# Two norms by factors spread to all partitions, with taps one a step and softmax sums in their own slot: a two-layer convolution and attention kernel on one core

## Chip, cores and metric

One NeuronCore of a Trainium2 chip. The metric is the device time of one execution in microseconds (us), lower is better. Times are medians over the executions of a kernel. A ratio is the mean time of one kernel's fast runs over the mean of the other's fast runs of the same rounds, so it is not quite the ratio of the medians beside it. Each ratio has a 95% interval.

## The reference

Four images of 128 channels and 64x64 pixels go through two layers. Cut to what matters here:

```python
# layer 0: norm over channels, 3x3 depthwise convolution added, window attention
y = _layernorm2d(x, ln_g, ln_b)            # mean and variance over the 128 channels of a pixel
y = y + _cpe(y, cpe_w, cpe_b)
xw = y.reshape(...)                        # 64 windows of 16x16 pixels
q, k, v = einsum(xw, Wq), einsum(xw, Wk), einsum(xw, Wv)     # 2 branches, 4 heads
attn = softmax(logits over a 5x5 neighbourhood)
x = x + Wo-projected attention output
# layer 1, on tokens [B, 4096, 128]
t = t + linear_attention(layernorm(t))     # running sums over the tokens
t = t + recurrent_ffn(layernorm(t))        # first step: Wx = layernorm(t) @ W.T, then a scan
```

Two norms are touched: the one at the head of layer 0, and the one ahead of `Wx`, called "W's norm" here. In both the mean and the variance are over the channels.

## The kernel before

The image is worked in 16 bands of 16 rows, four windows to a band, so 64 windows. A norm's mean and variance come most easily with pixels on the partitions (rows) and channels along the free axis, but the matmuls want channels on the partitions. So the kernel before scales the rows on VectorE (DVE) and turns them on TensorE (PE):

```python
    def normed(found, tiles, tag):                     # DVE, one instruction for each 128 pixels
        pieces, mv, rs = found
        xn = tiles.tile([P, 4, P], F32, tag=tag, name=tag)
        for j, piece in enumerate(pieces):
            nc.vector.tensor_scalar(
                xn[:, j, :], piece, mv[:, j, 0:1], rs[:, j : j + 1], ALU.subtract, ALU.mult
            )
        return xn

    def turned(xn, j0, n):                             # PE, one transpose for each 128 pixels
        tps = bank()
        for j in range(n):
            nc.tensor.transpose(tps[:, j * P : (j + 1) * P], xn[:, j0 + j, :], ident)
        return tps
...
    def turn_last(h):
        h.xl = p2.tile([P, 512], F32, tag="xl2", name="xl2")
        nc.scalar.copy(h.xl, turned(h.xn, 0, 4))

    def product(h):
        wps = bank()
        nc.tensor.matmul(wps, fwT, h.xl, start=True, stop=True)
        nc.scalar.copy(wx[:, h.b, h.hb], wps.rearrange("p (k s) -> p s k", s=SEG))
```

The softmax sums of a window take two small DMA trips: `dc` gathers 4 rows of sums to all partitions for a quick inverse, `rd` and `rden` send the inverses back and spread them. In the kernel before this is done one window (a "slot" of some 12.5 us) after the exponentials, and the product with the inverses (`oT`) another slot later:

```python
    def weighted(w):                                   # in the slot after the window's logits
        ops, dps = bank(), bank()
        # ... 4 sums of the exponentials on PE into dps
        nc.scalar.copy(den, dps)
        nc.sync.dma_start(dc, den[::HD, :])
        yield
        # ... 24 products with v on PE into ops
        yield
        nc.vector.tensor_tensor(dc, dc, pad_c, ALU.add)          # waits for the DMA of dc
        rc = a2.tile([P, 16], F32, tag="rc", name="rc")
        nc.vector.reciprocal(rc, dc)
        # ... two more small instructions
        nc.sync.dma_start(rd.rearrange("h (a e) -> (h a) e", e=16), rc)
        nc.sync.dma_start(rden, rd.unsqueeze(1).to_broadcast([HEADS, HD, BR * WT]))
```

Instructions of PE, DVE, ScalarE (ACT) and GpSimd (POOL) are held to program order. Those of SyncE (SP), which issues nearly every DMA, are not.

## Time and profile before

| | kernel before |
|---|---|
| time, first runs | 931.11 us (929.38 to 931.3, 3 runs) |
| profiled span, mean granted clock | 925.6 us, 0.981 |
| head (to the start of window 6) | 85.95 us |
| steady part (start of window 6 to that of window 63) | 712.3 us |
| tail (from the start of window 63) | 127.4 us |
| a band in the steady part | 50.2 us |

Windows and bands are counted from 0. The starts are those of the mask matmuls that open each window's logits.

### The profile page before, as it was taken

Reading aid. Unit: us, or ns where it says so; the run is one execution under the profiler, and the core shown is the slowest. Engines: PE = TensorE matmul, PEld = TensorE weight load, DVE = VectorE, ACT = ScalarE, POOL = GpSimd, SP = SyncE. Lnnn points to the kernel's source line nnn. Section 1 sums busy time; section 2 is a strip of 40 time slices with the busy share of each in tenths; the row PEclk is TensorE's granted clock in tenths of the full one; section 3 lists DMA queues with packets and bytes.
Section 4 is the critical chain, followed back from the end, with each engine's and each line's share of the span. In section 5 each row is a group of like instructions: output and inputs, shape, how many; then the busy total and the mean of one; then the engine's idle time right before and its main releaser. Section 6 shows DMA issues by size and latency. Waiting matters only on the chain.

```text
span 925.6 us, 26464 instructions
## 1 busy us (share of the span) xinstructions
PE 876.4 (95%) x10508; PEld 655.1 (71%) x10508; DVE 730.4 (79%) x2408; ACT 540.1 (58%) x1010; POOL 260.8 (28%) x358
## 2 busy tenths in 40 slices
PE   4978999999999999999999999999999999977894
PEld 3856777877777877777787777777777878665452
DVE  6464979888798878798888889787879887578684
ACT  3655656565756565665657575666666565623563
POOL 2122141423232232304132323323230412121195
PEclk9988999999999999999999999999999999989898
DMA  4112121122212121212112121212121111153254
GB/s 122 26 46 62 38 70 49 47 59 63 60 55 60 54 57 49 74 38 68 49 51 60 60 60 49 62 45 73 49 70 39 55 37 50 41 210 132 86 219 150
DMA packets 53189, 63.46 MB, mean 69 GB/s; under 512 B 22976, under 2 KB 33856, under 8 KB 52416
## 3 DMA queue, kind: packets, MB, share of 16 engines
q1 hardware_dynamic: 51616, 61.10, 21.1%
q8 instruction: 85, 1.39, 0.6%
q10 hardware_dynamic: 1440, 0.57, 0.2%
q14 instruction: 48, 0.39, 0.1%
HBM read 35.44 MB, written 17.30 MB: 57 GB/s over the span
## 4 chain that ended last, share of the span: by engine, by line
PE 61%; DVE 24%; ACT 5%; POOL 4%; issue 3%; DMA 2%; ACTq 0%; POOLq 0%; DVEq 0%; SPq 0%
PE bank L343 8%; DVE y L294 8%; PE bank L471 7%; PE bank L388 6%; PE bank L218 6%; PE bank L500 5%; PE bank L406 4%; PE bank L356 4%; PE bank L418 4%; PE bank L608 3%; DVE st L197 2%; PE z L834 2%; PE bank L579 2%; PE bank L543 2%; PE bank L581 2%
## 5 line engine op out<-in xcount | busy, mean ns | idle before, releaser
L294 DVE SCALAR_TENSOR_TENSOR y<-ypad,cpe_w,y 128x512 f32<-128x512 f32 x240 | 189.8, 791 | 17.1 <-ACT y L292 13.6
L397 ACT ACTIVATE es<-bank 128x512 f32<-128x512 f32 x256 | 132.2, 602 | 77.0 <-PE bank L388 77.0
L446 POOL TENSOR_TENSOR oT<-o_sb,rden 128x512 f32<-128x512 f32 x64 | 83.9, 1311 | 242.7 <-DMA rden<-rd 138.4
L201 POOL TENSOR_SCALAR rs<-mv 128x4 f32<-128x4 f32 (+2 forms) x100 | 25.1, 251 | 366.5 <-DVE mv L199 163.2
L209 DVE TENSOR_SCALAR xn<-x,mv,rs 128x128 f32<-128x128 f32 x256 | 89.9, 412 | 26.6 <-POOL rs L202 26.6
L202 POOL TENSOR_TENSOR rs<-rs,mhalf 128x4 f32<-128x4 f32 (+2 forms) x100 | 106.3, 1063 | 8.3
L388 PEld LDWEIGHTS bank<-q,k 32*128 32x128 f32 x3072 | 97.7, 189 | 7.5 <-ACT k L351 6.3
L388 PE MATMUL bank<-q,k 32*128 32x96 f32 (+1 forms) x3072 | 96.3, 270 | 1.1 <-ACT k L351 1.1
L418 PEld LDWEIGHTS bank<-es,v_sb 128*32 128x32 f32 x3072 | 56.6, 110 | 30.2 <-issue 20.2
L471 PE MATMUL bank<-woT,oT 128*128 128x128 f32 x512 | 68.0, 289 | 5.8 <-POOL oT L446 5.8
L471 PEld LDWEIGHTS bank<-woT,oT 128*128 128x128 f32 x512 | 64.8, 202 | 9.9 <-POOL oT L446 7.5
L500 PE MATMUL bank<-xl,awT 128*128 128x512 f32 x128 | 70.0, 630 | 0.0
L418 PE MATMUL bank<-es,v_sb 128*32 128x96 f32 (+1 forms) x3072 | 69.9, 239 | 0.0
L406 PE MATMUL bank<-es,ones 128*32 128x512 f32 x512 | 69.1, 612 | 0.0
L363 ACT COPY v_sb<-bank 128x512 f32<-128x512 f32 x64 | 37.6, 587 | 53.6 <-PE bank L356 44.6
L343 PE MATMUL bank<-y2w,wqT 128*128 128x256 f32 x256 | 67.3, 386 | 1.0 <-DVE y2w L294 1.0
L343 PE MATMUL bank<-y2w,wkT 128*128 128x256 f32 x256 | 66.7, 384 | 0.0
L356 PE MATMUL bank<-wvT,y2w 128*128 128x256 f32 x256 | 66.0, 380 | 0.0
L351 ACT COPY q<-bank 128x512 f32<-128x512 f32 x64 | 37.7, 588 | 42.2 <-PE bank L343 40.2
L351 ACT COPY k<-bank 128x512 f32<-128x512 f32 x64 | 37.4, 584 | 37.6 <-PE bank L343 37.5
L197 DVE BATCH_NORM_STATS2 st<-x 128x6 f32<-128x128 f32 x256 | 55.5, 280 | 1.1
L343 PEld LDWEIGHTS bank<-y2w,wqT 128*128 128x128 f32 x256 | 46.0, 195 | 13.0 <-issue 7.2
(118 smaller groups left out, 1713.7 us busy)
## 6 DMA issues: line engine op xcount, KB each, us to landing
rden<-rd SPq DMA_DIRECT2D x64, 256.0 KB
v_sb<-v_sb SPq DMA_DIRECT2D x128, 64.0 KB
resd<-rs_o SPq DMA_DIRECT2D x32, 256.0 KB
out<-ot SPq DMA_DIRECT2D x32, 256.0 KB
xin<-in_xt SPq DMA_DIRECT2D x15, 512.0 KB
res<-resd SPq DMA_DIRECT2D x3, 2048.0 KB
late<-resd SPq DMA_DIRECT2D x2, 1024.0 KB
dc<-den SPq DMA_DIRECT2D x64, 8.0 KB
```

The source lines that it names most:

```text
L202: nc.gpsimd.tensor_tensor(rs[:, :n], rs[:, :n], mhalf[:, :n], ALU.pow)
L209: nc.vector.tensor_scalar(xn[:, j, :], piece, mv[:, j, 0:1], rs[:, j : j + 1], ALU.subtract, ALU.mult)
L294: nc.vector.scalar_tensor_tensor(y2, src, cpe_w[:, tap : tap + 1], y2, ALU.mult, ALU.add)
L343: nc.tensor.matmul(pps[:, br * WT : (br + 1) * WT], wT[:, br * P : (br + 1) * P], y2, start=True, stop=True,)
L356: nc.tensor.matmul(vps[:, e * 256 : (e + 1) * 256], y2[:, e * P : (e + 1) * P], wvT, start=True, stop=True,)
L388: nc.tensor.matmul(sps[h][:, cols], w["k"][rows, k0 : k0 + P], w["q"][rows, cols], start=False, stop=(br, n) == pieces[-1],)
L397: nc.scalar.activation(es, sps[h], AF.Exp, scale=scale)
L406: nc.tensor.matmul(dps[rows], ones[:, :HD], w["es", h], start=True, stop=True)
L418: nc.tensor.matmul(ops[rows, cols], w["v"][:, n, c0 : c0 + HD], w["es", h][:, cols], start=(br, n) == pieces[0], stop=(br, n) == pieces[-1],)
L446: nc.gpsimd.tensor_tensor(oTs[n][:, :, :, wj * WS : (wj + 1) * WS], w["o"].rearrange("p (a r c) -> p a r c", a=BR, c=WS), w["rden"].rearra ...
L471: nc.tensor.matmul(yps[:, j * P : (j + 1) * P], oT[:, br, t], woT[:, br, :], start=br == 0, stop=br == BR - 1,)
L500: nc.tensor.matmul(zps, awT[:, m * P : (m + 1) * P], h.xl, start=True, stop=True)
```

## The change

The intent is to take the turning of layer 0's rows and of W's rows off PE, and their scaling off DVE. The host hands over x a second time with channels on the partitions (`xc`). The factors (1/sigma and mean/sigma of each pixel) are measured on rows as before, sent to DRAM, and read back spread to all 128 partitions. POOL then multiplies and subtracts on `xc`. W's norm needs only 1/sigma, as the mean is taken out by centring the weights once; the W product runs on the residual stream that is turned anyway, and DVE multiplies the result with the spread 1/sigma. Beside this: one tap of the convolution a step (a step is one of the 21 small portions into which the work ahead on a band is cut), where the second half of a band had two; sums in the window's own slot; SP in the program order too; the last, unused states dropped; six buffers for `ys`. The core of the diff:

```diff
-ENGINES = [... for e in ("PE", "DVE", "Activation", "Pool")]
+ENGINES = [... for e in ("PE", "DVE", "Activation", "Pool", "SP")]
...
+    class Group:                       # up to 4 x 128 pixels of a band
+        def measure(self):
+            # ... bn_stats, bn_aggr on DVE, three small POOL instructions -> self.both [P, 2, 4]
+            nc.sync.dma_start(self.x[:, : self.k * P], ins["xc"][b, wi, :, ...])
+        def send(self):
+            self.there = dram4.tile([2, P, self.k], F32, tag=f"both_d{self.k}", name="both_d")
+            nc.sync.dma_start(self.there.rearrange("f p j -> p f j"), self.both[:, :, : self.k])
+        def spread(self):
+            nc.sync.dma_start(
+                self.all[:, :, : self.k * P],
+                self.there.rearrange("f p j -> f (p j)").partition_broadcast(P),
+            )
+        def scale(self):
+            nc.gpsimd.tensor_tensor(x, x, self.all[:, 0, : self.k * P], ALU.mult)
+            nc.gpsimd.tensor_tensor(x, x, self.all[:, 1, : self.k * P], ALU.subtract)
...
-        yield from taps(y2, y, half * 2 * WS, 2 * WS, 1 + half)
+        yield from taps(y2, y, half * 2 * WS, 2 * WS, 1)
...
+    def send(h):                       # W's norm
+        nc.sync.dma_start(h.there, h.found[2])
+    def spread(h):
+        nc.sync.dma_start(h.rs, h.there.rearrange("p j -> (p j)").partition_broadcast(P))
     def product(h):
-        nc.tensor.matmul(wps, fwT, h.xl, start=True, stop=True)
-        nc.scalar.copy(wx[:, h.b, h.hb], wps...)
+        nc.tensor.matmul(wps, fwT, h.xs..., start=True, stop=True)
+        nc.vector.tensor_tensor(wx[:, h.b, h.hb]..., wps..., h.rs..., ALU.mult)
...
+            cuts = [(0, 4), (4, 8), (8, 9)] if wi == 0 else [(1, 5), (5, NCH + (wi < NB - 1))]
+            for e, (j0, j1) in enumerate(cuts):
+                g = Group(n, j0, j1)
+                at(k0 - 6 + e, g.measure)
+                at(k0 - 4 + e, g.send)
+                at(k0 - 2 + e, g.spread)
+                at(k0 + 1 + min(e, 1), g.scale)
+                at(k0 + 3 + min(e, 1), g.evict)
...
     for i in range(len(places) + 2):   # the slots
         logits(windows[i])
+        to_rows(windows[i - 1])        # rden read back
         weighted(windows[i - 1])
+        sums(windows[i])               # PE sums, dc sent
         window_inputs(windows[i + 1])
+        scaled(windows[i - 1])         # oT, most of a slot earlier than before
+        if i == len(places):           # the 6 MB read for the scan, one slot earlier
+            nc.sync.dma_start(res[:, b]..., resd[b])
+        inverses(windows[i])           # dc awaited, rd sent
```

The first band of an image is cut into three groups, the third of one chunk of 128 pixels; every other band into two.

## The prediction

> **What bounds the kernel now.** First the page, for busy shares and slices.
>
> ```profile
> PE 876.4 (95%) x10508; PEld 655.1 (71%) x10508; DVE 730.4 (79%) x2408; ACT 540.1 (58%) x1010; POOL 260.8 (28%) x358
> ...
> PE   4978999999999999999999999999999999977894
> ...
> DVE  6464979888798878798888889787879887578684
> ...
> PEclk9988999999999999999999999999999999989898
> ```
>
> TensorE (PE) is busy from end to end at a full clock, except in slices 2 and 3 (46 to 92 us) and 35 to 38. But a busy PE is not one at its peak, so I went on to the timeline of PE. The mask matmuls (L383) open each of the 64 windows; from their starts a band (4 windows) takes 50.2 us (121.67 to 774.11 us is 13 bands). Two of its slots take 11.2 and 11.6 us in every band: there each group of matmuls starts the moment the one before has streamed. The other two take 13.1 to 14.5 us; there PE has small holes, and the busy column hides most of them, since it models the tail of each matmul:
>
> ```profile
> 364.12 1.16 PE L543 MATMUL bank<-f,f 128*128 128x128 f32 x8
> 365.11 0.38 PE L218 MATMUL bank<-ident,x 128*128 128x128 f32 x2
> 365.69 0.59 PE L218 MATMUL bank<-ident,x 128*128 128x128 f32 x2 [0.20 <-DVE x L593]
> 366.12 1.03 PE L343 MATMUL bank<-y2w,wqT 128*128 128x256 f32 x4
> ...
> 370.68 1.01 PE L218 MATMUL bank<-ident,xn 128*128 128x128 f32 x4
> 371.53 0.39 PE L579 MATMUL bank<-v,aT 128*128 128x129 f32 x2
> ```
>
> Four transposes take 0.44 us from start to the next group (331.16 to 331.60 in the chain in order of time). Here the four of x take 1.0 us and the four of xn 0.85 us, because VectorE (DVE) is late. Adding each group's undisturbed length in the slot from 358.29 to 372.52 (14.23 us) gives 12.9 us; in the slot after it 13.2 of 13.3 to 13.8. So a band has some 48.6 us of matmul work and 1.6 us of holes made by DVE. PE bounds it, DVE is second in half of each band.
>
> Last, the DMA queue near the end:
>
> ```profile
> 815.37 0.54 SPq L437 DMA_DIRECT2D rden<-rd  x1
> 819.66 0.32 SPq L599 DMA_DIRECT2D resd<-rs_o  x1
> 822.27 1.27 SPq L724 DMA_DIRECT2D res<-resd  x3
> 845.98 6.53 SPq L599 DMA_DIRECT2D resd<-rs_o  x2
> ```
> ```profile
> 825.00:830.00 5.00, 4.53 (x27) 4.37 (x25) 2.44 (x12) 0.59 (x1) 1.20 (x2) 0.67 0.99 423
> 830.00:835.00 5.00, 4.36 (x14) 1.86 (x15) 4.25 (x18) 2.55 (x4) 1.20 (x2) 1.00 1.00 424
> 835.00:840.00 5.00, 4.80 (x30) 3.47 (x31) 4.41 (x9) 2.03 (x4) 0.00 (x0) 1.00 0.76 318
> ```
>
> The last two columns are DMA share and GB/s. Reading back the residual of three images (6 MB) fills every DMA engine from about 823 to 839 us. Before, nothing that computes needs a DMA in that time.
>
> **What the Trainium skill says.** (1) "DMA: Bandwidth & Descriptors", "Why a DMA increments its semaphore by 16 and not by 1": a DMA uses the largest number of engines up to 16 that divides the slowest dimension of both sides. The broadcast of the inverse sums (rden) is read with 4 heads outermost, so 4 engines. The trace agrees: DMA share 0.27 at 102 GB/s from 402 to 403 us. The new broadcasts have 128 outermost on both sides, so 16. (2) Same page, "Queues, rings and completion order": an engine consumes a queue's descriptors in ring order. The chain agrees; the same 8 KB copy takes 1.88 us alone and 4.57 us when issued right behind an rden:
>
> ```profile
> 40.04 1.88 DMA dc<-den
> ...
> 53.26 4.57 DMA dc<-den
> ...
> 70.94 5.18 DMA rden<-rd
> ```
>
> (3) "SBUF — State Buffer", "Who interferes with whom": a DVE instruction with two SBUF inputs and a GpSimd (POOL) instruction that reads SBUF block each other. The trace agrees: the 128x16 add on dc has a median of 164 ns and a maximum of 1257, and at 49.36 us it ends as the Pool multiply does. (4) "TensorE: Matmul & The Clock Gate", "Part 1": an idle window of about 3.4 us halves the clock. The trace agrees: 0.50 from 65 to 70 us, after PE waited 4.0 us.
>
> **Part by part: steady state.** Removed on PE:
>
> ```profile
> L218 PE MATMUL bank<-ident,xn 128*128 128x128 f32 x256 | 46.2, 289 | 5.1 <-DVE xn L209 4.8
> ...
> L218 PE MATMUL bank<-ident,xf 128*128 128x128 f32 x128 | 22.4, 296 | 9.8 <-DVE xf L209 9.7
> ```
>
> Half the xn ones go (128; those before W) and 119 of xf (band 0 keeps its 9). I don't use the mean of 289, which is latency: at 0.11 us of stream each it is 14.1 + 13.1 = 27.2 us. Four state updates (8 instructions at 0.11) give 0.9. Per band: 0.88 + 0.95 = 1.83 us.
>
> DVE: 128 xn scalings at 0.28 (4 take 1.11 us) = 36 us, and 119 of xf at about 0.27 = 32 us, go. Added are 32 products of PSUM with the spread factor, 0.69 us each as the like adds L478 show: 22 us. Net -46 us, 2.9 per band of some 42. ACT loses 32 turning copies (18.8 us) and 32 of wx (20.1). POOL gains two multiplies of 128x512 per group, 60 in all at 1.28 us (the oT multiply's median), plus some 8 us of small ones: 261 to about 345 us, far from a bound. But each of these 1.28 us can hold up a tap (L294 reads two SBUF tensors); 4.8 us a band, perhaps half of them met: +2.4 us, which eats most of DVE's gain. What remains is order: taps one a step rather than in pairs, sums in the window's own slot, so fewer bunches on DVE. I take the holes to fall from 1.6 to 0.8 us. A band then takes 48.6 - 1.83 + 0.8 = 47.6 us, 2.6 less; from 86 us (window 6) to 798 us there are 14.25 bands: **-37 us**.
>
> DMA grows by 8.4 MB of x in the other layout, 16 MB of spread norm factors and 8.4 MB of spread W factors: 63 to 96 MB, share 21% to some 32%. Steps are about 2.2 us apart; a factor sent waits two, a spread three (6.6 us). Two short copies took 1.9 and 1.7 us; 512 KB at the 423 GB/s above is 1.2 plus that, some 3.5. It fits.
>
> **Head.** From the starts of L383, windows 1 to 4 take 6.3 to 6.8 us, window 5 takes 25.1 (60.86 to 85.95). Its work is about 11 us. The loss is six taps in a row (DVE, 59.4 to 64), the late rden (5.18 us), PE waiting 2.8 us for oT, and the halved clock. The change multiplies oT most of a slot earlier and spreads the taps, so most of 14 us should go; but band 1's new norm has two DMA trips and 5 us of POOL, which I see ready only about when window 4 needs it. I take **-9 us**.
>
> **Tail.** Gained: PE waits from 817.6 to 822.3 us for the last oT; its chain dc, rd, rden starts a slot earlier now. From window 63's start the old output product came at +24 us, the new at about +16.5. Lost: the DMA issue is now held to program order, and the 6 MB read is issued right after the last oT, ahead of the spread of the factors of the last half but three. That spread cannot land before the read's 19 us are over (+35.5, then 1.5). DVE stands at the product that needs it, and the next norm is behind it in order: +39 us against +31 before (829.41). With the cold clock after it: **+9 us** net. The last product swaps a scaling, a turn and a copy for a send and a spread: level. The six buffers of ys: the adds on POOL run back to back (28 in 33.92 us), so -0.5 at most.
>
> Sum: 931 - 37 - 9 + 9 - 0.5, some **893 us**.
>
> **Rivals.** (a) DVE and POOL bind: each Pool multiply blocks the taps fully, DVE reaches 45 us a band and the long slots stay near 13.5; only half of the 37 us comes: 912. For it: 791 ns mean of the tap against 750 undisturbed. Against: DVE has 8 us of room a band before. (b) DMA order binds in steady state too: a send that waits for POOL stops the queue's issue, v and rden come late, PE waits: 925 or more. Against: v has a whole slot of slack. (c) The tail's read does not hold the spread (a different allocation, or the spread slips ahead): no +9 but -5, 879. (d) The head stall goes wholly and holes vanish: 880.
>
> **Range and chances.** Steady -25 to -46, head -14 to +2, tail -5 to +14; together 879 to 911 holds it 8 times in 10. Faster by 2% is under 912.5: 0.86. Within: 0.12, rivals (a) with a bad head, or (b). Slower: 0.02.
>
> **What would show it.** Starts of L383: bands of 47 to 48 us, long slots near 12.3; PE still the most busy; L218 at some 265 matmuls (128 of x, 128 xn, 9 xf); Pool near 345 us; taps' mean over 791 ns; window 5 under 16 us. In the tail: a DVE wait of 10 us or more for the spread factor at the W product while the DMA share is 1.0, and a clock of 0.5 to 0.7 after it. I am wrong if bands stay at 50 us, if PE waits on v, rden or y2w in steady state, or if the W product waits nowhere.

## More of the kernel before

A line of the waits names the waiting engine and line, what it waited for, then us in total, times, and the longest.

```profile
DVE dc L429 <- DMA dc<-den: 7.1, 4, 3.0
...
SPq L437 <- DMA rd<-rc: 50.6, 45, 1.9
```

DVE waits for `dc` only four times in the whole run, because the products with v lie between its sending and its use.

## The result

The kernel after the change is slower: 955.89 us (955.69 to 956.41, 4 runs) against 930.25 (927.49 to 931.3, 4 runs) in the same rounds, ratio 1.0281 (1.0257 to 1.0306). The results are correct. By parts, from the same window starts:

| part | before | after | difference | predicted |
|---|---|---|---|---|
| head | 85.95 | 90.43 | +4.5 | -9 |
| steady part | 712.3 | 718.2 | +5.9 | -37 |
| tail | 127.4 | 146.1 | +18.7 | +9 |
| span | 925.6 | 954.7 | +29.1 | -37.5 |

The page after:

```profile
PE 859.8 (90%) x10254; PEld 640.7 (67%) x10255; DVE 691.1 (72%) x2191; ACT 523.1 (55%) x954; POOL 351.6 (37%) x457
...
PE   4996999699999999799999997999999999836794
...
PEclk9998999799999999899999998999999999869798
...
q1 hardware_dynamic: 79824, 93.09, 34.6%
```

The work went as planned: PE has 254 instructions fewer, DVE 39 us less, POOL 91 us more. What is new are single weak slices of PE in the middle (slices 8, 17 and 25, counting from 1), with a lower clock beside each. There is one ahead of each of the images 2 to 4. The groups that answer to those shown of before:

```profile
L378 DVE SCALAR_TENSOR_TENSOR y<-ypad,cpe_w,y 128x512 f32<-128x512 f32 x240 | 182.0, 758 | 18.6 <-ACT y L376 17.7
...
L707 DVE TENSOR_TENSOR wx<-bank,rs_b 128x512 f32<-128x512 f32 x32 | 33.5, 1048 | 43.9 <-DMA rs_b<-rs_d 32.2
```

And the waits of DVE and PE:

```profile
DVE dc L500 <- DMA dc<-den: 71.3, 17, 14.2
...
DVE wx L707 <- DMA rs_b<-rs_d: 32.2, 8, 14.8
...
PE bank L235 <- DVE x L684: 26.0, 14, 7.6
PE bank L235 <- DVE xn L226: 15.5, 2, 14.9
```

DVE's wait for `dc` has grown from 7.1 to 71.3 us. DVE is in order, so all that is behind the addition to `dc` waits too; among it is `x L684`, the residual of layer 1, which PE then turns (L235).

From window to window the steady part shows where. Undisturbed slots are 11.6, 11.2, 12.4 and 12.1 to 12.6 us, a band of 47.3 to 47.8, as predicted (47.6). But three windows, 13, 29 and 45, take 22.79, 20.58 and 21.02 us. Each is the second of an image's last band, and just ahead of it the factors of the next image's first band, the one with three groups, are sent and read back. Other slots take 13 to 15.6 us. Together they add some 44 us, the three alone some 27; so a band stayed at 50.4 us on average. Here is the DMA queue (SP) ahead of the first of the three and in it, start and length in us, and then DVE and PE:

```profile
162.47 1.62 SPq L288 DMA_DIRECT2D both_d<-both  x1
...
166.05 7.23 SPq L294 DMA_DIRECT2D all<-both_d  x2
173.51 0.58 SPq L511 DMA_DIRECT2D rden<-rd  x1
...
175.57 0.69 SPq L494 DMA_DIRECT2D dc<-den  x1
...
181.96 0.58 DVE L500 TENSOR_TENSOR dc<-dc,pad_c 128x16 f32<-128x16 f32 x1 [8.64 <-DMA dc<-den]
...
183.65 0.73 PE L235 MATMUL bank<-ident,x 128*128 128x128 f32 x2 [7.61 <-DVE x L684]
```

SP stands between the two spreads at 166 us. Of that, 6.5 us are one wait of SP for the landing of the third group's send (`both_d`, issued at 162.47). The sums were ready at 169.27 us, but `dc` is issued only at 175.57, behind the third spread, `rden` and another store. It lands another 6.39 us later, DVE waits 8.64 us, PE 7.61, and PE's clock falls to 0.51 from 182 to 190 us.

The tail is as foretold. The last lines of the queue ahead of it, and the two waits:

```profile
828.84 1.27 SPq L875 DMA_DIRECT2D res<-resd  x3
...
831.42 0.51 SPq L694 DMA_DIRECT2D rs_b<-rs_d  x1
...
849.38 1.02 DVE L707 TENSOR_TENSOR wx<-bank,rs_b 128x512 f32<-128x512 f32 x1 [14.82 <-DMA rs_b<-rs_d]
851.43 1.24 PE L235 MATMUL bank<-ident,xn 128*128 128x128 f32 x4 [14.92 <-DVE xn L226]
```

The spread of W's factors, issued right behind the 6 MB read, is needed while the read fills the engines.

### The profile page after: what moved, and what is told of

The parts are those of the page before. It is cut to its first block, busy times and chain, and to the rows that moved or that the text cites.

```text
span 954.7 us, 26138 instructions
## 1 busy us (share of the span) xinstructions
PE 859.8 (90%) x10254; PEld 640.7 (67%) x10255; DVE 691.1 (72%) x2191; ACT 523.1 (55%) x954; POOL 351.6 (37%) x457
## 5 line engine op out<-in xcount | busy, mean ns | idle before, releaser
L378 DVE SCALAR_TENSOR_TENSOR y<-ypad,cpe_w,y 128x512 f32<-128x512 f32 x240 | 182.0, 758 | 18.6 <-ACT y L376 17.7
L215 POOL TENSOR_SCALAR rs<-mv 128x4 f32<-128x4 f32 (+1 forms) x67 | 25.5, 381 | 240.5 <-DVE mv L209 228.7
L561 PE MATMUL bank<-woT,oT 128*128 128x128 f32 x512 | 73.6, 304 | 8.5 <-POOL oT L536 8.5
L561 PEld LDWEIGHTS bank<-woT,oT 128*128 128x128 f32 x512 | 70.3, 217 | 13.2 <-POOL oT L536 8.9
L489 PE MATMUL bank<-es,ones 128*32 128x512 f32 x512 | 75.0, 605 | 2.2 <-ACT es L481 2.2
L427 PE MATMUL bank<-y2w,wqT 128*128 128x256 f32 x256 | 73.2, 409 | 1.0 <-DVE y2w L378 1.0
L521 PE MATMUL bank<-es,v_sb 128*32 128x96 f32 (+1 forms) x3072 | 72.6, 244 | 1.1 <-DMA v_sb<-v_sb 1.1
L500 DVE TENSOR_TENSOR dc<-dc,pad_c 128x16 f32<-128x16 f32 x64 | 18.1, 283 | 71.5 <-DMA dc<-den 71.3
L216 POOL TENSOR_TENSOR rs<-rs,mhalf 128x4 f32<-128x4 f32 (+1 forms) x67 | 67.3, 1004 | 5.6
L707 DVE TENSOR_TENSOR wx<-bank,rs_b 128x512 f32<-128x512 f32 x32 | 33.5, 1048 | 43.9 <-DMA rs_b<-rs_d 32.2
L435 ACT COPY k<-bank 128x512 f32<-128x512 f32 x64 | 37.5, 586 | 44.8 <-PE bank L427 44.8
```

What stands on the lines that cost most here:

```text
L216: nc.gpsimd.tensor_tensor(rs[:, :n], rs[:, :n], mhalf[:, :n], ALU.pow)
L378: nc.vector.scalar_tensor_tensor(y2, src, cpe_w[:, tap : tap + 1], y2, ALU.mult, ALU.add)
L427: nc.tensor.matmul(pps[:, br * WT : (br + 1) * WT], wT[:, br * P : (br + 1) * P], y2, start=True, stop=True,)
L489: nc.tensor.matmul(dps[rows], ones[:, :HD], w["es", h], start=True, stop=True)
L521: nc.tensor.matmul(ops[rows, cols], w["v"][:, n, c0 : c0 + HD], w["es", h][:, cols], start=(br, n) == pieces[0], stop=(br, n) == pieces[-1],)
L561: nc.tensor.matmul(yps[:, j * P : (j + 1) * P], oT[:, br, t], woT[:, br, :], start=br == 0, stop=br == BR - 1,)
```

## The experiments

All eighteen ran correctly, in the fast state but for one execution told below. "Kernel after" has 955.89 us and the ratio 1.0281 throughout. The first theories were: **A**, the bytes of the spread factors load the DMA queue, so that `dc` lands late; **B**, SP's program order holds `dc` back. D and E came later; each text says what its theory expects.

### The order of SP, and who issues dc

```diff
-ENGINES = [... ("PE", "DVE", "Activation", "Pool", "SP")]
+ENGINES = [... ("PE", "DVE", "Activation", "Pool")]           # e1
-        nc.sync.dma_start(w["dc"], den[::HD, :])
+        nc.scalar.dma_start(w["dc"], den[::HD, :])             # e2
```

> The changed kernel, with the DMA issues no longer held to program order (the list of ordered engines as before the change). Theory A (the 8 KB copy of the sums waits in the rings behind the 512 KB spreads, the rden broadcast and the residual writes, and DVE stands at it): little changes in the steady state, DVE's waits for dc stay at 50 to 75 us in total, the time stays within 1.5% of 956. Theory B (program order holds the issue itself back, the 3.6 to 6.3 us between the end of den and the issue of dc): the issues come right after den, the three 20 us windows shrink to 14 or so, the time falls to about 925. The tail: if the 6 MB read is still issued ahead of the spread, the 14.8 us wait for rs_b stays under both.

Measured: 987.95 us, ratio 1.0609 (1.0569 to 1.065). The order of the four computing engines is unchanged by the edit; only SP's differs.

```profile
DVE dc L500 <- DMA dc<-den: 93.6, 17, 9.9
```

Theory B falls in this form: the order as a whole saves 32 us.

> The changed kernel, with the copy den to dc issued by ACT on its own DMA queue. Theory A (ring order behind the bulk transfers): the copy lands in 2 to 3 us rather than 5 to 7, DVE's waits for dc fall from 71 us to under 15, the windows of 20 us go, the time falls by 30 to 40 us to about 920. Theory B (late issue): nearly as good, since ACT issues it at once, but then e1 must gain as well. Rival C (the 16 engines themselves are full, whatever the queue): the copy still takes 5 us or more and the time stays within 1%. The tail's 14.8 us wait for rs_b stays under all.

Measured: 942.47 us, 1.0138 (1.01 to 1.0176). The long windows shrink to 18.8, 17.8 and 17.1 us, and don't vanish. The `dc` for which DVE waits ahead of them still takes 4.6 to 5.2 us from issue to landing (6.4 to 7.0 in the kernel after), and ACT issues it 0.6, 3.1 and 3.5 us after the sums; what ACT waits for is told with e15. The Trainium skill, "DMA: Bandwidth & Descriptors", "Issuing engines are not separate DMA queues", says that copies from several issuing engines run on the same 16 DMA engines and that only issue time is saved. This agrees: a part is saved, the landing stays late.

### The 6 MB read one slot later

```diff
             res = early.tile([P, B - 1, NH, SEG, HSEGS], F32, name="res")
+        if i == len(places) + 1:
             for b in range(B - 1):
                 nc.sync.dma_start(res[:, b]..., resd[b])
```

> The changed kernel, with the 6 MB residual read issued after the spread of the second half's factors of the last band but one, rather than ahead of both spreads. If the 14.8 us wait of DVE for rs_b in the tail comes from the read ahead of it in the rings: that wait falls under 4 us, PE's 14.9 us hole goes, the clock does not drop after it, and the time falls by 15 to 19 us to about 938. If the spread is late for another reason (its own send), the wait stays over 10 us and the time too.

Measured: 938.17 us, 1.0101 (1.0054 to 1.0147).

```profile
DVE wx L707 <- DMA rs_b<-rs_d: 18.8, 7, 4.8
...
PE bank L235 <- DVE xn L226: 3.1, 5, 1.2
```

The longest wait for the spread falls from 14.8 to 4.8 us, PE's from 14.9 to 1.2, and 18 us are back. The tail falls from 146.1 to 128.9 us, so its mechanism is shown, and its size: all but 1.5 us of the +18.7.

### The inverses' broadcast on sixteen DMA engines

```diff
-        nc.sync.dma_start(w["rden"], w["rd"].unsqueeze(1).to_broadcast([HEADS, HD, BR * WT]))
+        for h in range(HEADS):
+            nc.sync.dma_start(
+                w["rden"][h * HD : (h + 1) * HD], w["rd"][h].partition_broadcast(HD)
+            )
```

> The changed kernel, with the broadcast of the inverse sums issued as four DMAs of 32 rows, each read 32 times with 32 outermost, so that each may use 16 engines rather than 4. If the rings of the four engines that rden uses are the slow part of the queue (3.2 us of 5 to 7 that dc takes to land): dc lands in some 3 to 4 us, DVE's waits for dc fall to 30 us or less, the time falls by 15 to 30 us. If the 512 KB spreads are what holds the copy, dc still takes 5 us or more in the long windows and the time falls by less than 8 us; three more issues a window (0.5 us each) may even cost some.

Measured: 939.95 us, 1.0087 (1.0044 to 1.0129). DVE's wait for `dc` falls to 44.8 us in total. In the windows where DVE waits, `dc` now lands 1.9 to 3.7 us after its issue rather than 5 to 7: it stood behind the slow broadcast on its four engines. But ahead of the three long windows `dc` is issued 5.5 to 7.7 us after the sums were ready, and these windows stay at 19.5, 17.4 and 16.8 us. So two delays are in a row, issue and landing, and this mends the second.

### Each norm turned as before, in the new schedule

e4 gives `Group` the bodies of the kernel before, with empty `send` and `spread`; e5 does the same to W's norm; e7 takes both.

```diff
         def scale(self):                               # e4
-            nc.gpsimd.tensor_tensor(x, x, self.all[:, 0, ...], ALU.mult)
-            nc.gpsimd.tensor_tensor(x, x, self.all[:, 1, ...], ALU.subtract)
+            self.xn = normed(self.found, a2, ...)
         def evict(self):
+            rows = turned(self.xn, 0, j1 - j0)...
...
-    def spread(h): nc.sync.dma_start(h.rs, ...)        # e5
+    def spread(h): nc.scalar.copy(h.xl, turned(h.xn, 0, 4))
```

> The changed kernel and its schedule, with layer 0's norm of bands 1 to 15 done as before (scaled on DVE, turned on PE, out of PSUM), W's norm still by the spread factor. The transposes cost PE 0.95 us a band, 14 us in all. If the 512 KB spreads and their sends are what makes dc late in the steady state: DVE's waits for dc fall from 71 us to under 20, the windows of 20 us go, windows 5 and 6 of the head too; the time falls by 44 + 5 - 14, some 30 us or more, to about 925. If dc is late because of rden and the rest, it stays near 956 + 14. The tail's wait for rs_b stays.

Measured: 921.35 us, 0.9911 (0.9883 to 0.9939). DVE's wait for `dc` is 28.7 us, most of it in the head; the three windows that were long are 13.2 to 14.1 us. Layer 0's factors cost 35 us net in the kernel after.

> The changed kernel and its schedule, with W's norm done as before (scaled, turned, product, copied by ACT), layer 0's norm still by spread factors. PE pays 0.88 us a band, 14 us. Gone: the 14.8 us wait in the tail with its clock drop (19 us by the run with the read later) and the other waits of DVE for rs_b (17 us in all, in some windows). If the tail is all of it: 956 - 19 + 14 = 951. If W's spreads (256 KB each, two a band) also help to make dc late, the time falls to 940 or under. The windows of 20 us should stay.

Measured: 935.7 us, 1.0061 (1.0035 to 1.0087). The long windows stay at 21.6, 20.8 and 20.8 us, so W's factors don't make them. The time is under the 940 that was set for W's spreads to help to make `dc` late, and DVE's wait for `dc` falls from 71.3 to 52.5 us. By parts, the tail is 24 us shorter, and the steady part 5.4 us longer, where 0.88 us a band would be 12.5. So most of the gain is the tail's, and W's spreads delay `dc` a little too.

> The new schedule alone (taps one a step, sums in their own slot, inverses and broadcast spread over the slot, DMA issues in program order, six buffers of ys), with both norms turned as before. If the loss is all the DMA traffic of the factors: no window of 20 us, no wait for rs_b, bands of 47.4 + 1.8 = 49.2 us against 50.2 before, the time some 10 to 20 us under the kernel before, 910 to 920. If the schedule itself lost time (sums that wait for exp, buffers taken from q, k, o), it is level with before or slower.

Measured: 918.13 us, 0.9869 (0.9841 to 0.9897). The new schedule alone, without any spread factor, is 1.3% better than the kernel before.

### Mends together

> The changed kernel with the three mends together: dc on ACT's queue, rden on 16 engines, the 6 MB read later. Alone they gave 13.5, 16 and 18 us. If dc's lateness is ring order and issue together, each single mend left the other half in place, and together they take the windows of 20 us away: 956 - 18 - 40 = about 898, and faster than before by over 3%. If the first two hit the same part of it, the sum is 956 - 18 - 20 = 918.

This is the kernel after with e2's, e3's and e6's edits: 915.76 us (910.88 to 919.3), 0.9834 (0.9796 to 0.9872). That is near the 918 set for two mends that hit the same wait. Windows of 16.5, 15.7 and 18.4 us remain. In them even ACT issues `dc` 2.9, 3.1 and 4.7 us after the sums.

The next two have layer 0's rows turned (e4) and the read later (e3); the second has `dc` on ACT too (e2).

> The changed kernel with layer 0's rows turned as before and the 6 MB read later; W's norm by the spread factor, in the new schedule. Additive from 921 (rows turned) and -18 (read later): 903 to 905, faster than before by 2.5 to 3%. If the tail's wait was partly the same thing as layer 0's spreads, less: 912.

Measured, five rounds: 904.44 us, 0.974 (0.9715 to 0.9764). Against e7 it says what W's factors are worth when the tail is mended: 14 us (12 by the ratios, as the two ran in different rounds).

> As e9_turned_read_later, with dc on ACT's queue too. DVE's waits for dc were 28.7 us with the rows turned, most of them in the head: if those are ring order, another 3 to 8 us; if not, level with e9.

Measured: 904.28 us, 0.973 (0.9702 to 0.9758), level. One of its four executions took 1671.35 us at a full clock; it was left out of the ratio, and it is unexplained.

### A quarter of the bytes

```diff
-                self.all[:, :, : self.k * P], self.there.rearrange("f p j -> f (p j)").partition_broadcast(P)
+                self.all[:, :, :P], self.there.rearrange("f p j -> f (p j)")[:, :P].partition_broadcast(P)
```

POOL reads these 128 columns for all four chunks. The values are wrong, though the result still passed the comparison.

> A wrong result on purpose: the changed kernel with every spread of layer 0's factors cut to its first 128 columns (512 B rows rather than 2 KB, 128 KB rather than 512 KB), the same number of DMAs, descriptors and issues; Pool multiplies the same shapes by them. If the bytes of the spreads in the rings are the cause: the windows of 20 us go, DVE's waits for dc fall under 35 us, and the time falls by most of 34.5 + 14 us, to 915 or less. If it is the number of DMAs, their descriptors or the program order in which SP must wait for each send: the time stays within 10 us of 956.

Measured: 943.87 us, 1.0168 (1.0146 to 1.0191), so 12 us of some 44; the windows stay at 21.3, 18.0 and 19.1. Theory A falls as the main cause. The profile shows what did not shrink. First SP's wait ahead of the long window, then a stretch within it (columns: busy time of PE, PE's weight loads, DVE, ACT and POOL, then granted clock, DMA share, GB/s):

```profile
SPq L294 <- DMA both_d<-both: 5.0, 1, 5.0
```
```profile
166.00:171.00 5.00, 5.00 (x37) 4.64 (x34) 3.14 (x10) 1.83 (x4) 3.62 (x4) 1.00 0.00 0
```

SP stands for the landing of 1 KB, and its second spread goes out at some 169 us. For the last 3 us of that wait, and 2 more, the records show the DMA engines idle. Nor is it the moving of the pieces: by the trace's records of DMA packets all 256 pieces of 4 bytes of this send start between 162.0 and 162.25 us, and its last landing event comes at 168.86. So it is more a latency than a load.

### The best with rows turned

> As e9_turned_read_later, with rden on 16 engines in four DMAs. If rden's 3.2 us on four engines is part of the waits in the head (dc 4.6 to 5.9 us behind it): another 4 to 8 us off; three issues more a window may take that back: level with e9.

e4's, e3's and e6's edits together: 896.29 us (895.44 to 897.59), 0.9658 (0.9637 to 0.968). This is the fastest of all, 3.4% under the kernel before.

### The third group's send and reading back drawn apart

Theory **D**: SP, in program order, stands at the third group's spread until its send has landed, and `dc` is behind it. If only the place is at fault, four steps in place of two between them should help.

```diff
-                at(k0 - 6 + e, g.measure)
-                at(k0 - 4 + e, g.send)
-                at(k0 - 2 + e, g.spread)
-                at(k0 + 1 + min(e, 1), g.scale)
+                at(k0 - 6 + min(e, 1), g.measure)
+                at(k0 - 4 + min(e, 1), g.send)
+                at(k0 - 2 + e + (e == 2), g.spread)
+                at(k0 + 1 + e, g.scale)
```

> Only the third, one-chunk group of each image's first band is moved: measured and sent one step earlier, spread and scaled one step later, so that four steps instead of two lie between its send to DRAM and the reading back. Theory D (SP, held in program order, stands at the reading back until the send has landed, 6.5 us in the window at 174 us, and dc waits in the order behind it): the three windows of 20 to 22 us fall to 12 to 15, the wait of SP at that line falls under 2 us each, dc's wait on DVE falls from 71 us to about 50, and the time by 15 to 22 us to 934 to 941 (ratio 1.004 to 1.012). Theory A' (the number and size of the transfers in those windows, whatever their place): the windows stay over 18 us and the time within 5 us of 956.

Measured: 967.5 us, 1.0441 (1.0396 to 1.0486). It is slower than the kernel after; the windows grew to 25.1, 24.6 and 24.9 us. Ahead of the first of them SP's wait moved to the next reading back, that of the inverses:

```profile
SPq L511 <- DMA rd<-rc: 11.6, 1, 11.6
```
```profile
163.04 0.53 SPq L506 DMA_DIRECT2D rd<-rc  x1
163.62 0.47 SPq L294 DMA_DIRECT2D all<-both_d  x1
175.81 0.58 SPq L511 DMA_DIRECT2D rden<-rd  x1
```

Two sends of factors were issued just before, at 159.04 and 160.23 us; the second, of the one-chunk group, landed only at 169.61. The inverses' send (`rd`) behind them took some 12 us to land; the same trip cost SP at most 1.9 us of waiting in the kernel before. The DMA share was 0.10 from 164 to 168 us. So D falls: whatever is read back behind the sends is late, wherever the spread stands.

The next two: the same edit with the later read and the sixteen engines, and the same again with `dc` on ACT.

> The same together with the late reading of the residual rows and the broadcast of the denominators by sixteen engines: every norm still by spread factors. If the three causes are separate (theory D), their gains add: 956 less about 18 (read later), 16 (sixteen engines) and 15 to 20, less some overlap of the last two: 902 to 912, ratio 0.972 to 0.982. If they share the same wait, it stays near 920 (the three mends without this one gave 915.8).

Measured: 936.81 us, 1.0085 (1.0046 to 1.0123), far over both expectations, with windows of 23.5, 24.7 and 23.6 us.

> The same with dc's copy issued by ACT. Theory D: SP no longer stands, so it makes little difference, within 4 us of the run before. If SP's order still holds dc back: 5 us or more faster.

Measured: 930.97 us, 1.0027 (0.9992 to 1.0062): 6 us better, so a part of SP's order remains, and ACT still issues `dc` 8.6 to 9.6 us after the sums in those windows. The trace puts ACT's wait in the first of them, 9.8 us, down to the landing of `rd`: the same slow trip, met from another engine.

The reason stands in the trace's semaphore events. The DMAs of SP and ACT share eight landing semaphores that they take in turn, and each issue comes after the landing of the DMA that had its semaphore before; among 591 such pairs in the kernel after and 783 in e15 there is no exception. In e15 `dc` takes the semaphore of `rd` ahead of all three long windows, and is issued 0.1 us after `rd` has landed (178.95 and 179.05, 383.26 and 383.36, 586.62 and 586.72). In e2 and e8 it is so with a copy of v or a spread in place of `rd`, again within 0.1 us. In the kernel after, the DMA that had `dc`'s semaphore ahead of each long window is the slow send itself. So issuing `dc` from another engine does not free it from the slow trip.

### The form of the send

Theory **E**: the send itself is slow to land and holds up what is behind it. The kernel writes, for each of 128 partitions and each of 2 factors, a piece of 4 to 16 bytes to a place of its own: 256 pieces. The edit stores a partition's factors side by side, in 128 pieces of 8 to 32 bytes, and POOL picks them with a stride. The Trainium skill, "DMA: Bandwidth & Descriptors", "Rules for kernel authors", advises to bring small transfers together; it has no number for a case like this one.

```diff
-            self.there = dram4.tile([2, P, self.k], ...)
-            nc.sync.dma_start(self.there.rearrange("f p j -> p f j"), self.both[:, :, : self.k])
+            self.there = dram4.tile([P, 2 * self.k], ...)
+            nc.sync.dma_start(self.there, self.both.rearrange("p f j -> p (f j)"))
...
-                self.all[:, :, : self.k * P],
-                self.there.rearrange("f p j -> f (p j)").partition_broadcast(P),
+                self.all[:, : 2 * self.k * P],
+                self.there.rearrange("p f -> (p f)").partition_broadcast(P),
...
+            f = self.all[:, : 2 * self.k * P].rearrange("c (p f j) -> c f p j", f=2, j=self.k)
```

> The kernel after the change with one thing else: the factors lie in DRAM as each partition has them (both factors of a partition together), so that a send has 128 pieces of 8 to 32 bytes in place of 256 pieces of 4 to 16, and both sides have the partition outermost; the spread reads the same bytes in one run. Theory E (the send itself takes long to land: in the windows of 20 us the queue stood for 5 to 9 us with the DMA engines' busy share at 0.00 to 0.16, and all that is issued behind the send, dc too, lands that much later): the three windows fall from 20 to 22 us to under 17, SP's longest wait behind a send falls from 6.5 us to under 4, and the time to 930 to 945 (ratio 1.000 to 1.016). If the send's form does not matter (rival: it is the fixed time of two DMAs one after the other, or the load on the queue): within 5 us of 956, windows over 19.

Measured: 932.09 us, 1.004 (1.0006 to 1.0073), 24 us less than the kernel after. The windows are 14.5, 16.1 and 14.5 us. In the stretch that had SP's 6.5 us wait, and the queue there:

```profile
SPq L295 <- DMA both_d<-both: 1.2, 1, 1.2
```
```profile
160.46 0.32 SPq L289 DMA_DIRECT2D both_d<-both  x1
...
163.20 2.03 SPq L295 DMA_DIRECT2D all<-both_d  x2
165.46 0.58 SPq L513 DMA_DIRECT2D rden<-rd  x1
...
167.28 0.57 SPq L496 DMA_DIRECT2D dc<-den  x1
```

From the third group's send to the spread that reads it is now under 5 us, not 11, and `dc` is issued the moment the sums are there (167.26). That the form of this trip makes the long windows is shown. The edit changed the spread's pieces too (one run in place of two for each partition), and no run separates the two; e11 speaks against the spread's bytes, not against the number of its pieces.

The landing events narrow it down. In the kernel after, the three sends of the one-chunk groups, in pieces of 4 bytes, land 10.4, 8.6 and 9.5 us after their issue begins. The other thirty have 256 pieces too, but of 12 or 16 bytes, and land in 1.6 to 4.0. In e16 the three, now in 128 pieces of 8 bytes, land in 4.3 to 4.4 us, in the same place behind another send. So it is not the number of 256 as such, and the sends themselves got faster, whatever the spread's pieces add. Whether the size of a piece or the smaller number did it is not separated.

> The same send with the late reading of the residual rows and the denominators' broadcast by sixteen engines: every norm still by spread factors. Theory E: 900 to 915, ratio 0.970 to 0.985. If the send's form does not matter: about 920, ratio 0.99.

Measured: 902.11 us (900.8 to 903.64), 0.9717 (0.9683 to 0.9751). Taken singly the three edits gave 24, 18 and 16 us, 58 in all; together they give 54. So the change as it was meant, all norms by factors, beats the kernel before by 2.8% once three transfers are mended.

### The head

> The kernel with the send by rows, the late reading and the sixteen engines, and the second band alone, whose norm falls into the head, turned on PE as before: all later bands and W by factors. If the 19.4 us before the last window of the head come from the factors' way there (the same kernel with all bands turned has 11.7), the head shortens by 6 to 8 us and the time falls from 902 to 893 to 897 (ratio 0.961 to 0.966), level with the best so far or a little under. If the head's wait has another cause, it stays within 3 us of 902.

Measured: 900.5 us, 0.9701 (0.9671 to 0.9732). The window before the steady part takes 17.8 us, hardly less than 19.4; e12 has 11.7. The head as a whole is 3.6 us shorter than in e17 (84.25 and 87.83), more than half of that before this window. So the second band's factors are not the main cause of the long one. DVE still waits 7.0 us for `dc` there, where e12 waits 1.7. In the queue, the third band's two sends and spreads stand just there, then SP waits for `rd`, and `dc` is issued at 70.42 us, 5.4 us after its sums. That points to the same trips of another band; no run took those away alone, so it stays open.

## Why the prediction was wrong

- **Steady part, the work.** Right: 1.83 us of PE work and some holes fewer a band made 47.6 of 50.2 us, and undisturbed bands take 47.3 to 47.8. Over 14.25 bands that would be the 37 us. (The four slots given add up to 48.9 us of matmul work a band, not 48.6; that is not what failed.)
- **Steady part, the DMA: here it failed.** The step is "Two short copies took 1.9 and 1.7 us; 512 KB at the 423 GB/s above is 1.2 plus that, some 3.5. It fits." It took the time of a short copy alone, in another form, for that of the one-chunk send in 256 pieces of 4 bytes, which landed 8.6 to 10.4 us after its issue and kept SP standing for up to 6.5; in e13 the store behind it cost SP 11.6. Then rival (b), "DMA order binds in steady state too", was dismissed with "v has a whole slot of slack". That is true of v, but the rival had to be tested on the transfer with the least slack. This is `dc`, which the same change had moved next to its use: a wait of 7.1 us in total became 71.3. The stalls added some 44 us and took the whole 37. Rival (b)'s "925 or more" is what came, though not by "a send that waits for POOL": SP waited for POOL's factors too (72.4 us in all, 4.0 at the longest), but e16 left these waits in place and brought the long windows down to 14.5 to 16.1 us.
- **rden's four engines** were read correctly from the skill (point 1 of the prediction), and their effect on the copy behind was even measured ("1.88 us alone and 4.57 us when issued right behind an rden"), but the sum charged nothing for it. It is worth 16 us in the new order (e6).
- **DVE and POOL.** DVE's load fell by 39 us, not 46: the product with the spread factor takes 1048 ns, not 690. ACT's fell by 17 us, not 39. POOL came to 351.6 us (predicted 345). The tap's mean fell from 791 to 758 ns where over 791 was expected, so the +2.4 us a band for blocked taps was not seen, and rival (a) went the other way. The blocking is real, but fewer taps met it: 4 of the 240 took over 1 us, all beside a POOL multiply, where before 15 did. In e17, without the stalls, the mean is 786 ns again.
- **Head.** Wrong: +4.5, not -9. The longest window of the head, window 5, takes 19.6 us where under 16 were expected; ahead of it DVE waits 9.6 us for the `dc` that now stands close to its use. With layer 0's rows turned, the sixteen engines bring the head from 85.1 us (e9) to 80.0 (e12), with that wait at 1.7. With the factors and the same mends it is 87.8 (e17). Which transfer of the factors delays `dc` there was not settled (e18).
- **Tail.** Right in mechanism, half in size: DVE's wait, PE's hole and the cold clock came at the place named. The norm behind the W product began at +42.4 us after window 63's start (predicted +39), and the output product only at +20.2, not +16.5. So of the 7.5 us to be gained there, 3.8 were, and +18.7 came in place of +9. e3 gives 17.1 of it back.
- **The chances.** 0.02 for slower was far too little. Rival (b) had no number of its own for the landing of a send, and none of `dc`'s slack.

Where the gain went, then: the undisturbed bands did get some 2.6 us shorter, and three transfers took it back: the factors' send (24 us), the read in the tail (18) and the four-engine broadcast (16). With them mended the kernel stands at 902, some 9 us above the prediction; its head is 1.9 us longer than before, where 9 were to be gained. And layer 0's factors, mended, bring nothing over turned rows: e17 has 0.9717, e12 0.9658. What W's factors bring (14 us) and the schedule (12 us) is the whole of the lasting gain, beside the mended broadcast.

## What to carry to other kernels

When a change adds small DMA trips, list every transfer that shares the queue with its slack, and test the rival on the one with the least, not on the biggest; a step that both adds trips and draws a wait closer to its use needs both counted together. Give a store of factors the form that each partition writes as one piece, don't send a group so small that its pieces have 4 bytes, keep broadcasts on all engines, and put a large read where nothing small behind it is awaited. An idle DMA share doesn't say that the queue is free: look at what the issuing engine stands for, and at which earlier DMA has the landing semaphore that the next issue needs.

## What the Trainium skill lacked or had wrong

- "DMA: Bandwidth & Descriptors" gives a fixed cost of a DMA of some 2 us (its fit is of DMAs that GpSimd issues) and advises to join small transfers, but beside general words on small pieces it has no time for a small store of many pieces that is read back. Here 1 KB in 256 pieces of 4 bytes landed 8.6 to 10.4 us after its issue (in e11 partly at a DMA share of 0.00), where 3 or 4 KB in 256 pieces of 12 or 16 bytes took 1.6 to 4.0. In 128 pieces of 8 bytes it landed in 4.3 to 4.4, and the kernel was 24 us faster.
- The same page has the rule for the number of engines, but not what a four-engine broadcast costs the copies behind it: 8 KB landed in 5 to 7 us behind it and in 1.9 to 3.7 behind one on sixteen; 16 us in the kernel.
- The same page says that SP and ACT own separate rings; that did not free `dc` here, as the DMAs of both take eight landing semaphores in turn. In e15 ACT issued `dc` 8.6 to 9.6 us after the sums, 0.1 us after the landing of the `rd` that had its semaphore. What such a turn costs in time has no number there.
- "SBUF — State Buffer" says that a DVE instruction with two SBUF inputs and a POOL instruction that reads SBUF block each other. The traces agree, but how often the two meet in a kernel decides, and the page has nothing on that: POOL did 91 us more here, and taps of over 1 us (744 ns undisturbed) fell from 15 to 4 of 240.
